# A mixture-of-experts layer on one core: the second pair's shared down product in seven half-products, one fetch of the expert lists, and a reordered start and routing

## The chip, the cores and the metric

The kernel runs on one core of one Trainium2 chip. The metric is the time of one execution on the device in microseconds, smaller is better. Before the change the median of nine runs is 1002.9 us (1000.19 to 1004.2).

The core has five engines with queues of their own: PE (matrix products into PSUM, the accumulator memory of eight banks), DVE (vector arithmetic), ACT (scalar functions, copies and casts), POOL (constants, indirect transfers) and SP (here only issues transfers). Each works through its queue in order and waits on semaphores for the others. Transfers run on 16 DMA engines beside them.

## What is computed

Inputs: `x` (8 batches of 256 rows of 1024, so T = 2048 tokens), one adapter number for each batch, eight adapter matrices of 1024 x 1024, and the weights of a mixture of 16 experts with a shared expert. Cut to what matters:

```python
w = weight[adapter_ids]
y = jnp.einsum('bsi,boi->bso', x, w)              # cond: one adapter matrix per batch

gu_s = y @ shared_w_gate_up.T                     # 1024 -> 2 * 1024
g_s, u_s = jnp.split(gu_s, 2, axis=-1)
shared_out = silu(g_s) * u_s @ shared_w_down.T    # 1024 -> 1024

probs = softmax(y @ gate_w.T)                     # 16 experts
topk_vals, topk_idx = top_k(probs, 2)             # two experts per token, weights normalised
...                                               # each expert: 1024 -> 2*256, silu(g)*u, 256 -> 1024
out = x + moe_out + shared_out
```

Only the two chosen experts of each token are computed, with fixed capacities for each expert in order of load (`CAPS`, 256 to 304 rows); what overflows goes through a conditional tail that is not entered here.

## The kernel before

**Precision.** Every product is in float32 quality: a float32 matrix is split into a high part and a low part in PE's reduced float32 type (`split`, lines 79 to 81: ACT casts the high part, DVE subtracts to get the low one), and a product is three matmuls, high x high, high x low, low x high (`mm3`, lines 103 to 106; the same three in `product`, line 425). So each weight tile that is loaded (`load_w`, line 89: a 512 KB load on SP into one of four staging tiles `st`, then `split` into one of five tiles `hl`) costs one cast on ACT and one subtraction on DVE.

**Work that is tucked between loads.** `between` is a list; each call of `load_w` takes its first entry and queues that work behind the subtraction of this load on its engine (lines 97 to 100, `issue_after`). The program is otherwise traced in order and a scheduler sets the order of each engine's queue by a simulated timeline, so the trace's order can differ from that of the lines where dependences allow it.

**Stages, in order of time.**

- `cond(b)` (line 209), eight times: y = x_b times its adapter matrix; two loads of x and eight of the matrix, 96 matmuls of 128 x 512. Results leave to DRAM (`y_d`) on ACT's queue.
- The shared gate/up product for a pair of token groups (four groups of 512 tokens: groups 0 and 1 are the first pair, 2 and 3 the second) is class `Up` (line 374): Strassen's scheme over the pair in stages `stage_a` to `stage_d`, with sums of the inputs in `sums` and of the weights in `sums_b` and `sums_d`. The first pair's sums of weights are stored in DRAM (`ss_d`) for the second. The first pair's stages alternate with `cond(3)` to `cond(7)`. y is read back (`y_block`, line 344, on POOL's queue) and transposed on DVE (line 178). `ring` holds four tiles of split operands. PSUM banks are taken in turn from seven (`bank`, line 75); the eighth bank is `psm`, for small things.
- `route(g, parts)` (line 236) for each group: 16 matmuls for each column part against the gate weights into `lp`, softmax, the two best experts, ranks, and eight indirect stores on POOL (line 333) that put token numbers and weights into a table `tab_d` in DRAM. For groups 1 to 3 the operands are split into `rb` tiles from the pool of `hl` (`parts_of`, line 363); for groups 2 and 3 the rows are transposed into the two halves of one tile `tt` first (`pair_work`, `transposed_pair`).
- After the last route: the order of the experts by load (lines 782 to 793), then `entries` (line 660): for each expert one small load of its token numbers (`tb`, line 670) and one of its weights (`cr`, line 671) on SP, first for the two first experts, later for the other 14. `places` makes gather indices of `tb` with a DVE transposition and four POOL additions (line 656); `weights` transposes `cr` on PE (line 683) into `ct`.
- `shared_down(g, h, ring, acc, dst)` (line 533): down product of one group: two halves of the output columns, four loads of `sd` each, 96 matmuls a half over four banks, then an addition into `acc` (line 554) and a store on SP (line 555). It runs for groups 0 and 1 here, while POOL gathers the rows of the first experts (line 579).
- Experts (lines 839 to 857): gathered rows, transposed, up product, down product.
- The second pair's `Up`, which reads the stored sums of weights, while `combine` (line 558) gathers and adds the expert rows for each group into `ca` tiles on POOL; then `shared_down(2, ...)` and `shared_down(3, ...)`, lines 894 and 895, and the kernel ends with the last four stores.

```python
    combine_kept(range(NB, 2 * NB))
    ...
    acc = combine(pc[1], range(2 * NB, 3 * NB), x)
    for u in range(4):
        up.stage_d(u)
    close(px)
    pd = pool("pd", 4)
    acc3 = combine(pd[1], range(3 * NB, 4 * NB), x)
    shared_down(2, G, ring, acc, out)
    shared_down(3, S_, ring, acc3, out)
```

Of the kernel before, what the change touches and what calls it, by code (L numbers as in the profile page):

```python
# [17 lines left out]
P = 128  # L18
B, S, H = 8, 256, 1024
T = B * S  # L20
# [3 lines left out]
G = 4  # L24
GT = T // G
# [5 lines left out]
SLOTS = T + CAP  # L31
# [6 lines left out]
def adapter_moe_kernel(ctx: ExitStack, tc: tile.TileContext, xT, x, itok, wc, gate, wgu, wd, sgu, sd, out):  # L38
# [45 lines left out]

    homes, loads, last_gather, marks = [whl], [0], [None], []
# [3 lines left out]
    def load_w(src, parts=1):  # L89
# [3 lines left out]
        for i in range(parts):  # L93
            cs = slice(i * 1024 // parts, (i + 1) * 1024 // parts)
            last_load[0] = nc.sync.dma_start(st[:, cs], src[:, cs])
            end = split(hl[:, 0, cs], hl[:, 1, cs], st[:, cs])
# [5 lines left out]

    def mm3(ps, lhs, rhs, first, last):
        nc.tensor.matmul(ps, lhs[0], rhs[0], start=first, stop=False)  # L104
        nc.tensor.matmul(ps, lhs[0], rhs[1], start=False, stop=False)  # L105
        nc.tensor.matmul(ps, lhs[1], rhs[0], start=False, stop=last)  # L106
# [4 lines left out]
    gpk = cpool.tile([P, NC * 2 * E + P], FR, tag="gpk", name="gpk")  # L111
# [3 lines left out]
    nc.sync.dma_start(it_sb, itok)  # L115

    ident = cpool.tile([2 * E, 2 * E], F32, tag="ident", name="ident")
# [9 lines left out]
    c1, c2 = (t[:, :, 1:2].bitcast(F32).rearrange("p a o -> p (a o)") for t in tid)  # L127
    msum = cpool.tile([P, E], BF, tag="msum", name="msum")
# [3 lines left out]
    def constants(ring):  # L132
        make_identity(nc, ident)
# [3 lines left out]
        nc.gpsimd.memset(ones, 1.0)  # L137
# [30 lines left out]
    def zeros(ys):  # L168
        zr = ys.tile([P, 1024], F32, tag="yr", name="zr")
        nc.gpsimd.memset(zr, 0.0)  # L170
        nc.sync.dma_start(y_d[T // P].rearrange("a p f -> p a f"), zr[:, :].rearrange("p (a f) -> p a f", a=4))
        nc.sync.dma_start(comb_d[T : T + P, :], zr[:, :E])
        nc.sync.dma_start(os_d[ZROW : ZROW + 16, :], zr[:16, :])
# [19 lines left out]
    def pair_work(tb, ys):  # L193
        tv = tt.rearrange("p k (b n) -> p (k b) n", b=4)
        r = [y_block(tb + k, ys) for k in range(2)]
        return tv, [lambda k=k: transpose_to(tv[:, :, k * P : (k + 1) * P], r[k], 4) for k in range(2)]

    def transposed_pair(tb, ys):
        tv, works = pair_work(tb, ys)
        for work in works:  # L200
            work()
        return tv


# [4 lines left out]
    def cond(b, rows):  # L209
        xt = [load_w(xT[b, :, 0, :], 2 if b == 0 else 1)]  # L210
        aid = nc.values_load(it_sb[0:1, b : b + 1], engines=(mybir.EngineType.SP,), min_val=0, max_val=NA - 1)
        yrow = [rows.tile([P, 1024], F32, tag="yrow", name=f"yrow{k}") for k in range(2)]
        for h in range(2):
            ps = [bank() for k in range(2)]
            for q in range(4):
                if h == 0 and q == 1:
                    xt.append(load_w(xT[b, :, 1, :]))
                w = load_w(wc[ds(aid, 1), h * 4 + q].rearrange("a p f -> p (a f)"), 2 if b == 0 and h == 0 and q == 0 else 1)
# [17 lines left out]
    def route(g, parts):  # L236
        lp = psm.tile([P, GT], F32, tag="sm", name="lp")
        n0 = 0
        for get, n in parts:
            for c in range(NC):  # L240
                for l in range(2):
                    nc.tensor.matmul(  # L242
                        lp[:, n0 : n0 + n],
                        gpk[:, c * 2 * E : c * 2 * E + P],
                        get(c)[l],
                        start=(c == 0 and l == 0),
                        stop=(c == NC - 1 and l == 1),
                    )
            n0 += n
# [3 lines left out]
        for k in range(NB):  # L253
            nc.tensor.transpose(lt[:, k, :], ls[: 2 * E, k * P : (k + 1) * P], ident)
# [108 lines left out]
    def parts_of(srcs):  # L363
        for src in srcs:
            t = []
            for k in range(2):
# [618 lines left out]
```

## Time and profile before

| what | value |
|---|---|
| median of nine runs | 1002.9 us |
| the profiled execution | 1004.28 us, its span from first to last instruction 1002.4 us |
| mean granted clock of PE | 0.997 |
| busy: PE, DVE, ACT, POOL | 980.0, 661.3, 532.0, 304.8 us |
| DMA | 252.45 MB, 252 GB/s over the span |
| matmuls 128 x 512: from one start to the next | 0.227 us at full pace |
| DVE subtraction, 128 x 1024 | 1.22 us |
| ACT cast, 128 x 1024 | 1.05 us |
| DVE addition of a bank, 128 x 512 | 0.69 us |
| ACT copy of a bank, 128 x 512 | 0.59 us |

How to read the profile's lines. A timeline line gives start, duration, engine, line, operation, written tile and read tiles, shapes, how many are merged, and in brackets the idle time of the engine before it and what ended it. Matmuls are pipelined, so the duration of one (0.39 us) is longer than its distance to the next. A line of waits gives who waited for whom, the total, how often and the longest. A line of a stretch gives its bounds and length, then for PE, PEld (weight load), DVE, ACT and POOL the busy time with the number of instructions, then PE's granted clock, the share of the DMA engines and GB/s. A group line gives busy time, mean ns of one, and the idle time of the engine before them.

### The profile page before, as it was taken

To read this page: it belongs to the slowest core of one execution; us is meant where nothing else is said; L and a number is where in the kernel's file an instruction comes from. 1 tells how busy PE (TensorE), PEld (TensorE's weight loads), DVE (VectorE), ACT (ScalarE), POOL (GpSimd) and SP (SyncE) were. 2 spreads that over 40 slices of the span, in tenths; PEclk is the share of its full clock that TensorE was granted. 3 is DMA by queue.
4 is the path that set the end of the run, shared out by engine and by line. 5 is a ranking of instruction groups with operands and counts; after the bars stand their busy time and mean duration, and the time that the engine had idled before them with its cause. 6 is when DMAs were issued, how large, how long until landed. Compare 5 with 4: busy or idle time off the path is not lost.

```text
span 1002.4 us, 14185 instructions
## 1 busy us (share of the span) xinstructions
PE 980.0 (98%) x5043; PEld 839.5 (84%) x5043; DVE 661.3 (66%) x886; ACT 532.0 (53%) x709; POOL 304.8 (30%) x312
## 2 busy tenths in 40 slices
PE   6989999999999999989999999999999999999997
PEld 4878878888888888879999999999998888888886
DVE  5567588565876786848878778878875324565531
ACT  4546466556553451416777767767665556233220
POOL 1000303000003003847885664650003352603200
PEclk9999999999999999999999999999999999999999
DMA  8988647979878134749988888888878999946931
GB/s 286 332 292 301 211 148 219 393 268 319 273 216 291 62 126 118 252 150 367 332 301 299 259 296 293 275 283 305 298 245 300 262 331 323 273 139 200 265 124 44
DMA packets 83783, 252.45 MB, mean 252 GB/s; under 512 B 13367, under 2 KB 22199, under 8 KB 83703
## 3 DMA queue, kind: packets, MB, share of 16 engines
q1 hardware_dynamic: 51526, 174.07, 50.9%
q0 software_dynamic: 19312, 60.47, 20.8%
q10 hardware_dynamic: 12864, 16.91, 4.6%
q8 instruction: 41, 0.67, 0.3%
q14 instruction: 40, 0.32, 0.1%
HBM read 203.17 MB, written 48.25 MB: 251 GB/s over the span
## 4 chain that ended last, share of the span: by engine, by line
PE 85%; DMA 4%; POOL 3%; issue 3%; DVE 2%; SPq 1%; ACT 1%; ACTq 0%; POOLq 0%; DVEq 0%
PE acc L425 28%; PE acc L105 18%; PE acc L106 18%; PE acc L104 18%; PE acc L647 2%; POOL yg L579 2%; DMA st<-wc 1%; DVE hl L81 1%; PE lp L242 1%; POOL tab_d L333 1%; DMA y_d<-yrow 1%; DMA raw<-sgu 1%; ACT hl L80 1%; DMA st<-xT 1%; SPq L670 0%
## 5 line engine op out<-in xcount | busy, mean ns | idle before, releaser
L81 DVE TENSOR_TENSOR hl<-st,hl 128x1024 fp32r<-128x1024 f32 (+1 forms) x254 | 304.9, 1208 | 177.5 <-ACT hl L80 176.6
L80 ACT CAST hl<-st 128x1024 fp32r<-128x1024 f32 (+1 forms) x254 | 263.0, 1042 | 200.3 <-PE acc L106 79.7
L425 PE MATMUL acc<-op,hl 128*128 128x512 f32 x1056 | 242.6, 390 | 0.7 <-DVE hl L81 0.7
L425 PEld LDWEIGHTS acc<-op,hl 128*128 128x128 f32 x1056 | 197.5, 188 | 41.9 <-DVE hl L81 1.1
L579 POOL DMA_INDIRECT yg<-y_d,ix x128 | 160.3, 1252 | 57.9 <-issue 33.2
L104 PE MATMUL acc<-yte,hl 128*128 128x256 f32 (+6 forms) x512 | 147.4, 288 | 0.0
L106 PE MATMUL acc<-yte,hl 128*128 128x256 f32 (+6 forms) x512 | 147.3, 288 | 0.0
L105 PE MATMUL acc<-yte,hl 128*128 128x256 f32 (+6 forms) x512 | 146.9, 287 | 0.0
L105 PE MATMUL acc<-hl 128*128 128x512 f32 x256 | 100.9, 394 | 3.6 <-DVE hl L81 3.6
L105 PE MATMUL acc<-hl,ht 128*128 128x512 f32 x256 | 100.4, 392 | 0.0
L106 PE MATMUL acc<-hl,ht 128*128 128x512 f32 x256 | 100.2, 393 | 0.0
L106 PE MATMUL acc<-hl 128*128 128x512 f32 x256 | 100.1, 391 | 0.0
L104 PE MATMUL acc<-hl 128*128 128x512 f32 x256 | 91.9, 394 | 8.2 <-ACT hl L80 8.2
L104 PE MATMUL acc<-hl,ht 128*128 128x512 f32 x256 | 99.6, 392 | 0.0
L105 PEld LDWEIGHTS acc<-yte,hl 128*128 128x128 f32 x512 | 96.4, 188 | 0.6
L104 PEld LDWEIGHTS acc<-yte,hl 128*128 128x128 f32 x512 | 96.4, 188 | 0.6
L106 PEld LDWEIGHTS acc<-yte,hl 128*128 128x128 f32 x512 | 96.2, 188 | 0.0
L347 POOL DMA_DIRECT2D yr<-y_d x24 | 13.3, 554 | 249.6 <-DMA y_d<-yrow 139.4
L425 PE MATMUL acc<-op,shl 128*128 128x512 f32 x288 | 66.7, 389 | 0.0
L104 PEld LDWEIGHTS acc<-hl 128*128 128x128 f32 x256 | 48.3, 190 | 19.2 <-ACT hl L80 9.3
L425 PEld LDWEIGHTS acc<-op,shl 128*128 128x128 f32 x288 | 54.1, 188 | 11.2
L105 PEld LDWEIGHTS acc<-hl 128*128 128x128 f32 x256 | 48.3, 189 | 16.1 <-DVE hl L81 6.3
(191 smaller groups left out, 1321.0 us busy)
## 6 DMA issues: line engine op xcount, KB each, us to landing
st<-wgu SPq DMA_DIRECT2D x64, 512.0 KB
st<-wc SPq DMA_DIRECT2D x63, 512.0 KB
st<-sd SPq DMA_DIRECT2D x32, 512.0 KB
st<-wd SPq DMA_DIRECT2D x32, 512.0 KB
os_d<-o SPq DMA_DIRECT2D x32, 512.0 KB
yr<-y_d POOLq DMA_DIRECT2D x24, 512.0 KB, 5.3
st<-sgu SPq DMA_DIRECT2D x24, 512.0 KB
st<-ss_d SPq DMA_DIRECT2D x20, 512.0 KB
```

Of the source, the lines that this page charges most:

```text
L80: nc.scalar.copy(hi, src)
L81: return nc.vector.tensor_tensor(lo, src, hi.bitcast(F32), op=ALU.subtract).ins
L104: nc.tensor.matmul(ps, lhs[0], rhs[0], start=first, stop=False)
L105: nc.tensor.matmul(ps, lhs[0], rhs[1], start=False, stop=False)
L106: nc.tensor.matmul(ps, lhs[1], rhs[0], start=False, stop=last)
L242: nc.tensor.matmul(lp[:, n0 : n0 + n], gpk[:, c * 2 * E : c * 2 * E + P], get(c)[l], start=(c == 0 and l == 0), stop=(c == NC - 1 and l == 1),
L333: i = nc.gpsimd.indirect_dma_start(out=tab_d[:, :], out_offset=bass.IndirectOffsetOnAxis(ap=sli[:, k : k + 1], axis=0), in_=tid[r][:, tb, ...
L347: nc.gpsimd.dma_start(r, y_d[tb].rearrange("a (i t) f -> (a i) (t f)", t=4))
L425: nc.tensor.matmul(ps, lhs[x], rhs[y], start=(first and c == 0 and i == 0), stop=(c == 3 and i == 2), skip_group_check=True)
L579: last_gather[0] = nc.gpsimd.indirect_dma_start(out=r[:, t * 256 : (t + 1) * 256], out_offset=None, in_=y_d.rearrange("k a p f -> (k a p) f"),
L647: nc.tensor.matmul(ps, a3[:, fi, :], w[fi][:, l, hs], start=(fi == 0 and l == 0), stop=(fi == 1 and l == 1))
```

## The change

The diff does the following.

- **Second pair's down product** (new class `DownPair`). The two groups of tokens and the two halves of the output columns make a 2 x 2 block product, with the inner dimension halved as well; it is done by seven half-products of 48 matmuls (Strassen's scheme in Winograd's form, with 15 sums) in place of eight. Sums of weights and activations are made on DVE (`t1`, `t2`, `s3` between the loads of stage D; the others inside `run`), results that two blocks share are copied from PSUM by ACT (`copies`) and either copied back into fresh banks as a start value or added by DVE (`add`). The sums use the tiles `raw`, which are free by then. The last block's four stores go on ACT's queue.
- **One fetch of the expert lists.** `entries` is called once: one indirect load on POOL brings 320 entries for each expert into `cr`, repeated on all partitions, with row numbers `column` made on DVE (four small instructions); one DVE transposition and one DVE addition make all gather indices `ix`. The weights' transpositions on PE are three in place of six and are queued behind the newest matmul. `tab_d` is padded to a multiple of 320 slots an expert.
- **The start.** Twelve matmuls on constants (`warm`) come first. The first x tile and the first weight tile are loaded in halves in the order x, w, w, x (`load_first`), and the second half of x is loaded before the third weight tile of the batch and not before the second.
- **Later transpositions, routing in parts.** `route` is cut into `route_part` (16 matmuls for half of a group) and the rest. For groups 1 and 2 the halves and the rest become entries of `between`; for group 2 the rows' transpositions do, too. The three stores of zeros go to POOL's queue. The first pair of loads for `sums_b(0)`, the gate weights and the table's start values are queued behind the newest load.

```diff
+    def load_first(xsrc, wsrc):
...
+        for k, i in ((0, 0), (1, 0), (1, 1), (0, 1)):
+            src, st, hl = pieces[k]
+            cs = slice(i * 512, i * 512 + 512)
+            with tc.issue_after(last_load[0].ins):
+                last_load[0] = nc.sync.dma_start(st[:, cs], src()[:, cs])
+            split(hl[:, 0, cs], hl[:, 1, cs], st[:, cs])
...
+    nc.gpsimd.memset(ones, 1.0)
+    warm = psm.tile([P, 4, P], F32, tag="sm", name="warm")
+    for k in range(12):
+        nc.tensor.matmul(warm, ones, ones[:, :].rearrange("p (o n) -> p o n", o=1).to_broadcast([P, 4, P]), start=True, stop=True)
...
-                if h == 0 and q == 1:
+                if h == 0 and q == 2:
                     xt.append(load_w(xT[b, :, 1, :]))
...
+    class DownPair:
+        def __init__(self, h, raw):
+            self.h = [[h[n][:, 4 * k : 4 * k + 4, :] for k in range(2)] for n in range(2)]
+            self.r = [raw[n][:, 4 * k : 4 * k + 4, :] for n in range(2) for k in range(2)]
...
+        def works(self):
+            return [lambda f=f, t=t: f(t) for f in (self.t1, self.t2, self.s3) for t in range(2)]
...
+            ps = banks4()
+            self.product(ps, operand(ring, a11), self.weights(0, 0), True)
+            for t in range(2):
+                self.s12(t)
+            copies(a11, ps)
+            self.product(ps, operand(ring, a12), self.weights(1, 0), False)
+            s2 = operand(ring, r[1])
+            w = [made(self.flat(3, t)) for t in range(2)]
+            add(0, 0, ps)
+            store(0, 0, nc.sync)
+            ps = banks4()
+            for k in range(NB):
+                nc.scalar.copy(ps[k], a11[:, k, :])
+            self.product(ps, s2, w, False)
+
+            for t in range(2):
+                q = slice(2 * t, 2 * t + 2)
+                nc.vector.tensor_tensor(a12[:, q, :], a12[:, q, :], r[1][:, q, :], op=ALU.subtract)
+            copies(r[1], ps)
+            s3 = operand(ring, r[0])
+            w = []
+            for t in range(2):
+                x, y = self.loaded(1, 1, t), self.loaded(0, 1, t)
+                nc.vector.tensor_tensor(x, x, y, op=ALU.subtract)
+                w.append(made(x))
+            self.product(ps, s3, w, False)
+            copies(r[0], ps)
+            ops = operand(ring, a22)
...
+            self.product(ps, ops, w, False)
+            s1 = operand(ring, a21)
+            w = [made(self.flat(2, t)) for t in range(2)]
+            add(1, 1, [r[0][:, k, :] for k in range(NB)])
+            add(1, 0, ps)
+            store(1, 0, nc.sync)
+            ps = banks4()
+            self.product(ps, s1, w, True)
+            s4 = operand(ring, a12)
+            w = self.weights(1, 1)
+            add(0, 1, [r[1][:, k, :] for k in range(NB)])
+            add(1, 1, ps)
+            store(1, 1, nc.sync)
+            self.product(ps, s4, w, False)
+            add(0, 1, ps)
+            store(0, 1, nc.scalar)
...
+        nc.gpsimd.indirect_dma_start(
+            out=cr.rearrange("e s o -> e (s o)").bitcast(I32),
+            out_offset=None,
+            in_=tab_d.rearrange("(e s) o -> e (s o)", s=ENTRIES),
+            in_offset=bass.IndirectOffsetOnAxis(ap=column, axis=0),
+        )
+        nc.vector.transpose(ib, cr[:, :, 0].rearrange("p (t i) -> p t i", i=32))
+        nc.vector.tensor_scalar(ix, ib.rearrange("p t n -> p n t")[:, :E, :].bitcast(I32), seg[:, 0:1], None, op0=ALU.add)
...
-    places, weights = entries(pe[1], [0, 1])
-    places()
+    weights = entries(pe[1], column)
     e0 = expert_rows(pa[1], 0)
-    between[:] = [None] * 4 + [weights]
     shared_down(0, G, ring, down_rows(0, ys), xs_d)
     rs = expert_rows(pa[1], 1)
-    places, weights = entries(pe[1], range(2, E))
     yt, works = expert_yt_work(pa[1], e0)
-    between[:] = [works[0], None, works[1], places, works[2], None, weights]
+    between[:] = [None, weights, None, works[0], None, works[1], works[2]]
...
-    for u in range(4):
+    down = DownPair((G, S_), raw)
+    up.stage_d(0)
+    between[:] = down.works()
+    for u in range(1, 4):
         up.stage_d(u)
     close(px)
     pd = pool("pd", 4)
     acc3 = combine(pd[1], range(3 * NB, 4 * NB), x)
-    shared_down(2, G, ring, acc, out)
-    shared_down(3, S_, ring, acc3, out)
+    down.run(2, ring, (acc, acc3), out)
```

The routing's new order in the stream of loads:

```diff
+    between[:] = [w[0], w[1], w[2], both(w[3], part(0)), part(1), lambda: route(1, lp)]
     up.stage_a(0)
     up.stage_a(1)
-    route(1, parts_of([raw[1][:, :, k * 2 * P : (k + 1) * 2 * P] for k in range(2)]))
+    up.stage_a(2)
     zeros(ys)
-    up.stage_a(2)
+    after_loads(lambda: up.sums_loads(0))()
     up.stage_a(3)
...
-    tv, w = pair_work(2 * NB, ys)
-    between[:] = [None, None, None, w[0], None, None, w[1]]
+    lp2 = logits()
+    w = group_work(lp2, 2, ys)
+    between[:] = [None, None, None, w[0], None, None, w[1], None, None, w[2], both(*w[3:]), lambda: route(2, lp2)]
     cond(6, ys)
-    route(2, parts_of(tv if k == 0 else transposed_pair(2 * NB + k, ys) for k in (0, 2)))
```

## The prediction

> **What bounds the kernel now.** I read the page's busy shares first, then the list of waits for the matmul engine alone, then stretches of the timeline around each wait, and last the stretch that the change rewrites. The first line of the page says that PE is the path:
>
> ```profile
> PE 980.0 (98%) x5043; PEld 839.5 (84%) x5043; DVE 661.3 (66%) x886; ACT 532.0 (53%) x709; POOL 304.8 (30%) x312
> ```
>
> 98% says that a gain must come from fewer matmuls or from PE's few gaps. The waits of PE, all of them (engine, line, what it waited for: total us, times, longest):
>
> ```profile
> PE acc L104 <- ACT hl L80: 8.2, 2, 7.4
> PE acc L105 <- DVE hl L81: 3.6, 5, 1.8
> PE ct L683 <- DMA cr<-tab_d: 2.5, 1, 2.5
> PE lp L242 <- DVE rb L81: 0.9, 1, 0.9
> PE acc L425 <- DVE hl L81: 0.7, 1, 0.7
> PE lp L242 <- ACT rb L80: 0.3, 1, 0.3
> ```
>
> 16.2 us in all, of which 7.4 lie before the first matmul. One matmul's price is not the 390 ns of the groups (matmuls overlap) but the distance between two starts. The timeline of PE around the `ct` wait shows both that and what a wait does to the pace:
>
> ```profile
> 440.49 0.39 PE L106 MATMUL acc<-hl,ht 128*128 128x512 f32 x1
> 440.71 0.39 PE L104 MATMUL acc<-hl,ht 128*128 128x512 f32 x1
> 443.63 0.42 PE L683 MATMUL ct<-ident,cr 16*128 16x16 f32 x3 [2.53 <-DMA cr<-tab_d]
> ...
> 446.06 0.63 PE L104 MATMUL acc<-hl,ht 128*128 128x512 f32 x1
> 446.48 0.63 PE L105 MATMUL acc<-hl,ht 128*128 128x512 f32 x1
> 446.91 0.63 PE L106 MATMUL acc<-hl,ht 128*128 128x512 f32 x1
> ...
> 448.44 0.39 PE L105 MATMUL acc<-hl,ht 128*128 128x512 f32 x1
> 448.66 0.39 PE L106 MATMUL acc<-hl,ht 128*128 128x512 f32 x1
> ```
>
> Normal pace: 0.227 us. After 2.53 us of idleness eight matmuls start 0.427 us apart, so this wait costs 2.5 + 8 x 0.2 = 4.1 us. After the 1.84 us gap before 72.69 the pace is 0.23 at once: the half pace comes somewhere between 1.84 and 2.53 us.
>
> **The change, part by part.** Durations are from the profiled execution (1004.28 us, span 1002.4); its own time lies 1.4 above the median of 1002.9, so I sum there and take 1.4 off at the end.
>
> *Seven half-products.* The stretch from 909 to 996 is the second pair's down product:
>
> ```profile
> 909.00:996.00 87.00, 87.00 (x385) 71.88 (x383) 32.44 (x35) 17.93 (x18) 15.78 (x12) 1.00 0.56 165
> ```
>
> PE (first pair after the length) never idles, DVE is busy 32.4 of 87 us, ACT 17.9. Its groups (busy us, mean ns of one, idle before):
>
> ```profile
> L104 PE MATMUL acc<-hl,ht 128*128 128x512 f32 x128 | 49.8, 389 | 0.0
> L81 DVE TENSOR_TENSOR hl<-st,hl 128x1024 fp32r<-128x1024 f32 x12 | 14.7, 1222 | 22.3 <-ACT hl L80 22.3
> L554 DVE TENSOR_TENSOR ca<-acc,ca 128x512 f32<-128x512 f32 x15 | 10.1, 687 | 21.0 <-PE acc L106 21.0
> ```
>
> DVE's 22 and 21 us of idleness here are the room for the new sums. The loops give 384 matmuls; seven products of 48 are 336. The 48 that go are worth 48 x 0.2267 = 10.9 us. What comes beside them: DVE gets 14 operand splits, 14 weight splits and 10 half sums of 128x1024 at 1.22 (46.4) and 24 additions at 0.687 (16.5): 62.9 us in 76.2 of PE. ACT gets 28 casts at 1.05 and 16 copies at 0.59: 38.8. Three sums in halves (6 x 1.22 = 7.3 us of DVE) go to stage D, where from 850 to 910 DVE is busy 37.8 of 60. So on the average both fit; the question is the tightest product. S's last part ends at 913.86 now (L518 starts at 913.18); the four halves of `s12` (4.9) and one weight split (1.2) behind it end at 920.0, which is 909 + 10.9, where the first product ends. The second product writes the first bank then and the third bank 2.7 us later, and each needs a copy of 0.59 that in turn needs `s12`'s half: slack 2 us. Where a product goes on in the banks just copied, a bank is full 18 matmuls (4.1 us) before the product ends, and the copy or addition takes 0.6 to 0.7: covered, as long as ACT's or DVE's queue does not hold something late ahead of it. If that cover is gone in one product, it costs what DVE is over: the first window is the fullest, 12.5 us of work if nothing of it was done before, against 10.9. Bounds for new waits 0 (the stretch above, idle 0) to 7 x 1.6 = 11.2; I take 0.5, near the row with no wait, since DVE's queue keeps 13 us free. Loads are 12 of 512 KB plus six in stage D against 16: DMA share there is 0.56. The tail behind the last addition (996.20) has the same four additions and stores, on ACT's queue, which has nothing else left. **-10.9 + 0.5.**
>
> The Trainium skill (TensorE: Matmul & The Clock Gate, A second HAM failure mode: psum-queue depth-cycling) speaks against this part: cycling through PSUM banks can let PE idle briefly so often that its clock falls and rises again. The granted clock from 755 to 909, where copies and seeds alternate with products in the same way, is 1.00 and PE waits for nothing; were the rule to bite with eight slow matmuls in each product, the part would gain 1.6 x 7 = 11.2 less.
>
> *One fetch of entries.* 32 small DMAs on SP go (28 of them from 430.2 to 442.5, which held the `wgu` loads until 444.6), two memsets and eight small POOL instructions; the six transpositions become three, put behind the newest matmul. The wait for `cr` goes with its slow matmuls: **-4.1**. What comes: four small DVE instructions (0.17 to 0.42 each), one indirect DMA on POOL (L579: 1.25 us to issue, 5.6 to land for 128 KB; this is 320 KB, and other indirect rows take up to 13.5), one DVE transposition (0.44 for 256 elements, so about 0.55) and one DVE addition. Before, the scatter ended at 395.3 and the first gather began at 402.1; now 396.6 + 1.3 + 5.6 to 13.5 + 1 is 404 to 412, 2 to 10 later. The transpositions of the first expert sit three loads (16 us) later too, and its first matmul starts at 456.4: hidden, 0. Without that cover it costs the lateness itself, at most 10. POOL's later gathers queue behind the fetch but no longer wait until 446 for the second list: earlier. Below nothing I see only the 0.4 of three transpositions.
>
> The Trainium skill (TensorE: Matmul & The Clock Gate, Part 1) puts the fall of the clock after an idle window of about 3.4 us. Here 2.53 us were enough for eight matmuls at 0.427 us, and the measurement decides; by the rule alone the term would be 2.5.
>
> *The start.* Timeline of PE:
>
> ```profile
> 7.40 1.22 PE L104 MATMUL acc<-hl 128*128 128x512 f32 x2 [7.40 <-ACT hl L80]
> ...
> 12.96 0.73 PE L104 MATMUL acc<-hl 128*128 128x512 f32 x2 [0.79 <-ACT hl L80]
> 14.22 0.50 PE L105 MATMUL acc<-hl 128*128 128x512 f32 x1 [0.53 <-DVE hl L81]
> ```
>
> 14 matmuls take 6.82 us where 3.17 would do: 3.65 lost, by slow matmuls until 10.86, then by loads. Twelve matmuls on constants from about 1.2 us on, at 0.427, end near 6.3 and leave about one us of idleness: the pace should be full (were they as slow as one whole slow matmul, 0.63, they would end at 8.8 and cost 1.4). Order of the loads: the second half of the input (512 KB, cast at 10.62) goes behind the second weights (cast at 11.87), so these come about 1.3 us earlier, and 1 MB of `S<-sgu` (12.8, 13.8) and the writes that follow leave this stretch, where the DMA share is 0.86. Bounds 0 and -3.65; I take **-2.2**, since only the loads' part is sure to limit. The gap of 0.42 at 36.56 hangs, by the chain of waits, on a DVE sum of that early pair: **-0.4**. The gaps at 59.3 and 72.7 (0.9 and 2.0 with what follows) hang on DVE holding a transposition whose `yr` lands late; its place among the loads stays: 0, bounds -2.9 and +1. The pair's two loads now go behind stage A's weights, around 135, where the DMA share is 0.44; the sums that need them come after 175: 0 (if late, one `raw<-sgu` landing, 6.6). The three zero stores go from SP to POOL's queue (0.53 each), which is idle from 160 to 240 but for 8 us: 0. Gate and table loads move by some tens of us, ahead of the route that needs them at 78: 0.
>
> *Routing in parts.* Same matmuls, set between loads. The gaps are 0.43 + 1.14 at 268 and 269 (half two's transpositions start only after half one's splits) and 0.87 at 134. Bounds -2.4 and, if a part takes two of five `hl` buffers from the loads at a bad moment, +2 (as at 72.7). I take **-1.2**, half, as the second group's last transpositions are still one bundle.
>
> Sum: -10.9 + 0.5 - 4.1 - 2.2 - 0.4 - 1.2 = -18.3; 1004.3 - 18.3 = 986.0, against the median 984.6. **I predict 984.6.**
>
> **Rivals.** (a) *Loads bound the start and the parts trade waits*: start 0, routing 0, the 0.4 stays; -10.4 - 4.1 - 0.4 = -14.9, 988.0. For it: DMA share 0.86 to 0.90 until 75 us. Against it: over 1 MB leaves. (b) *DVE becomes the bound in the down product*: 11.2 of new waits rather than 0.5, 995.3; half of it 990. For it: 62.9 of 76 us and an in-order queue in which a sum waits for a load; against: it runs ahead. (c) *Slower*: at the product boundaries PE waits for ACT's copies (four casts behind a late sum, or 4 x 0.59 = 2.4 plus an addition of 0.69) and each wait passes the length at which PE falls to half pace. One costs 2.5 + 1.6 = 4.1 as at 443; the six boundaries 24.6, in place of the 0.5: 984.1 + 24.6 = about 1009. It decides from 18.3 / 6 = 3.1 us a boundary. Against: four banks fill 1.36 us apart, and from 755 to 909 no such wait. (d) *The parts do not do what they say*: the scheduler puts the route's matmuls together again; only the 1.2 goes: 986.
>
> **How the numbers follow.** Forecast with (d) 0.65, (a) 0.15, (b) 0.13, (c) 0.07. The lower end takes all bounds: 10.9 + 4.5 + 3.65 + 0.4 + 2.9 + 2.4 = 24.8, 978; the upper reaches to most of (b): 994. The measurement tells 0.2% (2 us) from no change. All but (c) lie below that; of their 0.93 I leave 0.03 to a mix that cancels: faster 0.90, same 0.03, slower 0.07.
>
> **What would show it.** Right: the seven products take about 76 us and PE's wait list has nothing from them; no wait at `ct` and no 0.427 pace near 443; first real matmul near 7.2 and full pace by 12; the lines at 268 without idle. Wrong: PE waits on DVE `shl` or ACT copies after stage D, PEclk below 1.00 there, or a POOL fetch that PE's first expert waits for.

## The result, and the profile after

The changed kernel takes 1010.1 us (median of 20 runs, 1004.7 to 1017.4) and the kernel before 1003.4 (62 runs, 1000.1 to 1007.3): a ratio of 1.0071, 95% interval 1.0057 to 1.0084. It is slower by 7 us, where 18 us of gain were forecast.

PE is still the path: busy 978.3 of a span of 1007.3 us, at a mean granted clock of 0.992. The change takes 48 matmuls away, and PE's list of waits shows where more than their worth went (the first four of its entries):

```profile
PE lp L269 <- ACT rb L82: 4.6, 1, 4.6
PE acc L486 <- DVE X L569: 3.8, 2, 2.2
PE acc L127 <- ACT hl L82: 3.0, 3, 1.7
PE acc L127 <- DVE acc L619: 2.9, 2, 2.6
```

In the list of before the longest wait behind the first matmul is the one at `ct`, 2.5 us, and that one is gone. In its place stand these: a part of the routing (line 269, `rb`), a bank in the stages C and D that DVE frees late (line 569), the start (line 127 for ACT's `hl`), and a bank that the shared addition frees late (line 619).

The part that the forecast worked out at most length behaves as forecast. The stretch of the new down product:

```profile
924.80:1001.00 76.20, 76.20 (x337) 62.76 (x335) 52.32 (x58) 30.39 (x39) 16.64 (x12) 1.00 0.57 158
```

PE is busy all of the 76.2 us at clock 1.00, DVE 52.3 of them and ACT 30.4. The forecast's 62.9 and 38.8 count the product's whole work; of its 38 sums and splits on DVE and its 28 casts on ACT, seven of each are done before the first matmul, and the last additions come behind the last one. From its first matmul to its last the product takes 76.2 us, against 86.8 before. But it begins at 924.8 us and not at 909.0. **The kernel had lost 15.8 us before its main part began.**

Where, by the ends of stages in three profiled executions (us; the second changed one is the run a0 below). An end is the start of the ACT or DVE instruction that takes the stage's last result; the last two rows are starts of matmuls:

| stage ends | before | changed | changed, a0 |
|---|---|---|---|
| `cond(0)`, its last copy | 33.7 | 31.8 | 33.6 |
| `cond(3)` | 106.8 | 105.1 | 109.0 |
| stage A, first pair | 159.3 | 164.0 | 167.7 |
| second step of stage B | 203.1 | 209.9 | 213.6 |
| stage D, first pair | 362.2 | 372.1 | 373.2 |
| shared down product, groups 0, 1 | 460.6 | 470.1 | 472.1 |
| first matmul of the last down product | 909.0 | 924.8 | 925.3 |
| last matmul | 995.8 | 1001.0 | 1001.2 |

So there are four places: from 106 to 159, from 159 to 372, around 447 (a loss that takes the old one's place), and stage D of the second pair. The first changed execution also lost 3.6 us at the end of the experts, which a0 did not; it is left out of what follows. How far one execution can be trusted: before, e1 and e7 below are the same kernel up to stage D of the second pair, and their profiles differ by up to 2.2 us at the ends ahead of it.

### The profile page after: what moved, and what is told of

Read it like the earlier page. It is cut to its first block, busy times and chain, and to the rows that moved or that the text cites. A ratio compares the mean times of both kernels' runs of the same rounds, so it can differ in the third digit from the quotient of the medians.

```text
span 1007.3 us, 13998 instructions
## 1 busy us (share of the span) xinstructions
PE 978.3 (97%) x5004; PEld 832.9 (83%) x5004; DVE 684.9 (68%) x915; ACT 542.7 (54%) x729; POOL 312.4 (31%) x314
## 5 line engine op out<-in xcount | busy, mean ns | idle before, releaser
L83 DVE TENSOR_TENSOR hl<-st,hl 128x1024 fp32r<-128x1024 f32 (+1 forms) x244 | 293.1, 1210 | 142.8 <-ACT hl L82 141.0
L82 ACT CAST hl<-st 128x1024 fp32r<-128x1024 f32 (+1 forms) x244 | 252.5, 1041 | 143.5 <-PE acc L129 59.1
L362 POOL DMA_INDIRECT tab_d<-tid,sli x32 | 40.0, 1249 | 143.6 <-DVE ranks L355 108.9
L486 PE MATMUL acc<-op,shl 128*128 128x512 f32 x288 | 68.8, 397 | 4.3 <-DVE X L569 2.2
L127 PEld LDWEIGHTS acc<-hl 128*128 128x128 f32 x256 | 47.7, 188 | 14.2 <-ACT hl L82 4.4
L128 PEld LDWEIGHTS acc<-hl 128*128 128x128 f32 x256 | 48.0, 188 | 13.5 <-DVE hl L83 3.6
L129 PEld LDWEIGHTS acc<-hl 128*128 128x128 f32 x256 | 48.1, 188 | 9.7
L82 ACT CAST yte<-tt 128x1024 fp32r<-128x1024 f32 (+6 forms) x43 | 35.8, 865 | 35.5 <-DVE tt L210 35.5
```

What stands on the lines that cost most here:

```text
L82: nc.scalar.copy(hi, src)
L83: return nc.vector.tensor_tensor(lo, src, hi.bitcast(F32), op=ALU.subtract).ins
L129: last_product[0] = nc.tensor.matmul(ps, lhs[1], rhs[0], start=False, stop=last).ins
L362: i = nc.gpsimd.indirect_dma_start(out=tab_d[:, :], out_offset=bass.IndirectOffsetOnAxis(ap=sli[:, k : k + 1], axis=0), in_=tid[r][:, tb, ...
L486: nc.tensor.matmul(ps, lhs[x], rhs[y], start=(first and c == 0 and i == 0), stop=(c == 3 and i == 2), skip_group_check=True)
```

## The experiments

Kernels that ran on the same chip share its runs of the kernel before. The chips differ: on two of the five here the kernel before takes 1003 to 1004 us, on three 1028 to 1032. On those three every profile has a stretch between 425 and 515 us in which PE stands idle between one matmul and the next, up to 2.9 us at a time, and waits for nothing that the profile shows. The stretch from 460 to 490 us of run e1 (columns as in the stretch above; before has 200 matmuls there, at clock 1.00) and one of run e9 show it:

```profile
460.00:490.00 30.00, 15.31 (x54) 11.97 (x55) 6.54 (x10) 3.49 (x7) 15.41 (x17) 0.60 0.58 189
```

```profile
476.00:494.00 18.00, 12.46 (x68) 9.56 (x67) 10.02 (x14) 8.04 (x14) 13.50 (x12) 1.00 0.69 219
```

The granted clock does not make the gaps: in e1 they begin at 460 and the clock falls at 465, in e9 it stays at 1.00. What makes them is open.

Ratios from those chips therefore have wide intervals, and there I go by the ends of stages ahead of that stretch, against run e1, which is the kernel before up to stage D of the second pair.

### First set: one part alone, or one part undone

**e1, the half-products alone**, in the kernel before:

```diff
+    down = DownPair((G, S_), raw)
+    up.stage_d(0)
+    between[:] = down.works()
+    for u in range(1, 4):
         up.stage_d(u)
...
+    down.run(2, ring, (acc, acc3), out)
```

> The kernel before with only the seven half-products (and their six pieces of work in stage D). Theory 1 (the half-products keep what was forecast, the loss lies in the other parts): 384 - 336 = 48 matmuls of 0.227 us less, 10.9, and one wait of some 1.8 us in stage D, as the trace of the change has it at 894.7, so about 1003.4 - 9.1 = 994.3, ratio 0.991. Theory 2 (the sums, their loads and their splits shift the queues and pay the saving back): 0.998 to 1.002.

Measured 0.9946 (0.9903 to 0.9989), between the two. The product takes 75.9 us, but in stage D PE waits 3.75 us at 913.6 and then runs 13 matmuls at half pace, 6.5 us in all. 10.9 - 6.5 = 4.4, and the ratio says 5.6.

**e3, the moved loads undone**, in the changed kernel:

```diff
-            if u:
-                self.sums_loads(u)
+            self.sums_loads(u)
...
-    after_loads(lambda: up.sums_loads(0))()
```

> The changed kernel with one thing undone: the first pair's two loads go back into sums_b. Theory 1a (these loads, issued at 104.5 beside the y round trip of the first pair and not at 135, make the stalls at 136 and, by the order of the later loads, at 194): the stalls of 7.3 and 2.2 us go, about 1010.1 - 6 to - 9 = 1001 to 1004, ratio to the kernel before 0.998 to 1.001. Theory 1b (the routing in parts makes them, since POOL's scatters now stand ahead of the last gathers of y): no change, 1009 to 1011, ratio 1.006 to 1.008.

Measured 0.9992 (0.9948 to 1.0037). The stall of the routing shrinks to 2.1 us and eight slow matmuls, 4.0 in all, where the next two runs on the same chip have 10 to 11.

**e4, the routing whole again**, in the changed kernel:

```diff
-    between[:] = [w[0], w[1], w[2], both(w[3], part(0)), part(1), lambda: route(1, lp)]
+    between[:] = up.rows_work(1)
     up.stage_a(0)
     up.stage_a(1)
+    route_whole(1, parts_of([raw[1][:, :, k * 2 * P : (k + 1) * 2 * P] for k in range(2)]))
```

(and likewise for groups 2 and 3).

> The changed kernel with the routing of groups 1, 2 and 3 whole again, in its old places. Theory 1b (routing in parts is the cause): the stall of 7.3 us at 136 goes and the old gap of 0.9 there and 1.6 at 268 come back: 1010.1 - 5 = about 1005, ratio 1.002. Theory 1a (the moved loads are the cause): within 1.5 us of the changed kernel, ratio 1.006 to 1.009.

Measured 1.0158 (1.0095 to 1.0221), and the stall is still there: 7.3 us at 137.8, 10.5 with what follows. So the routing does not make it. The ratio is above both theories.

**e5, the old fetches of entries**, in the changed kernel (the function itself as before, with its 32 small loads):

```diff
-    weights = entries(pe[1], column)
+    places, weights = entries(pe[1], [0, 1])
+    places()
...
-    between[:] = [None, weights, None, works[0], None, works[1], works[2]]
+    between[:] = [works[0], None, works[1], places, works[2], None, weights]
```

> The changed kernel with the two old fetches of entries (32 small transfers on SP, two lists) back. Theory 1c (the single fetch lands so late that the stall of 4.4 us at 447 only takes the place of the 4.1 at the old ct wait): within 1 us of the changed kernel, ratio 1.006 to 1.008. Rival (the late fetch also delays the experts' rows up to the end of the experts, where another 3.6 us were lost): 1010.1 - 4 = 1006, ratio 1.003.

Measured 1.0162 (1.0102 to 1.0223). Neither case gives this number; the wait at `ct` (2.0 us at 419) and the stalls at 140 (6.2) and 198 (1.4) are in its profile. That e4 and e5 stand above 1.007 is either the chip or the undone parts' worth, and the times alone do not say which.

### Second set

**a0, the changed kernel again.**

> The changed kernel itself, unaltered, beside the next three on one chip, since the chip of the first four experiments runs the kernel before at 1032 and not at 1003. If the runs with the routing back (1.016) and with the entries back (1.016) stand where they do because both still have the moved loads, this one is at 1.012 to 1.018 there; if undoing those two parts cost time by itself, it is at 1.006 to 1.008 as in the first comparison.

It came to a chip where before takes 1003.3, so it does not answer its question; it gives 1.0060 (1.0033 to 1.0087) and a second profile, which I use in the table above.

**e6, loads and routing both back** (e3 and e4 together).

> The changed kernel with both the two moved loads and the routing of groups 1 to 3 back. Theory 1 (the moved loads make most of the stall at 136, the routing in parts the 4 us that were left of it when the loads alone were back): that stall falls to some 1.3 us as in the kernel before, the gap of 1.6 at 268 comes back; 2 to 3 us below the run with the loads alone back, ratio 0.995 to 0.998. Rival (what is left there is the later start of the gathers of y, whatever the routing does): no gain, ratio 0.999 or more.

Measured 1.0036 (1.0012 to 1.0060): more than theory 1 said, on the rival's side. At 203 us it is 1.2 us behind before where a0 is 10.5, so the stretch from 106 to 203 is repaired. But 2 to 4 us go at 330, where no part that I had named is at work, and 6.3 in stage D of the second pair.

**e7, the half-products alone, t2's subtractions later than its loads** (the edit is shown against e1):

```diff
-            return [lambda f=f, t=t: f(t) for f in (self.t1, self.t2, self.s3) for t in range(2)]
+            return [lambda: self.t1(0), lambda: self.t1(1), self.t2_loads, None, lambda: later(0), lambda: later(1)]
```

(`t2_loads` holds the two loads, `later(t)` the subtraction of `t2` and `s3`.)

> The kernel before with only the seven half-products, and in stage D the two loads of the sum t2 one slot of the loop, the subtractions two or three slots later. Theory 1 (DVE stood 11.0 us behind that landing, PE 3.9 and 13 matmuls at half pace, 6.5 in all): the stall goes, 6 us below the half-products alone, ratio about 0.989. Rival (the half-products' sums and loads cost elsewhere): as before, 0.994 to 0.996.

Measured **0.9911 (0.9878 to 0.9944)**, 993.5 us: 9.9 less than before, on the faster kind of chip, and near theory 1. The stall was DVE standing, in order, before one landing. In the changed kernel and then in e7 (timeline, idle time and its cause in brackets):

```profile
892.81 1.22 DVE L648 TENSOR_TENSOR raw<-raw 128x1024 f32<-128x1024 f32 x1 [8.86 <-DMA raw<-sd]
893.96 0.68 DVE L569 TENSOR_TENSOR X<-acc,X 128x512 f32<-128x512 f32 x1
894.56 1.22 DVE L83 TENSOR_TENSOR hl<-st,hl 128x1024 fp32r<-128x1024 f32 x1
```

```profile
881.14 1.23 DVE L584 TENSOR_TENSOR raw<-raw 128x1024 f32<-128x1024 f32 x1 [2.23 <-DMA raw<-sd]
```

Behind the subtraction of `t2` stands the addition of line 569, which frees a bank that PE needs. The load may go out only when the old content of its tile has been split, so it cannot be early; its subtraction has to be late.

**e8, the start alone**, in the kernel before, with the change's `load_first`:

```diff
+    for k in range(12):
+        nc.tensor.matmul(warm, ones, ...)
...
+            x0, w0 = load_first(lambda: xT[b, :, 0, :], lambda: weights(0))
...
-                if h == 0 and q == 1:
+                if h == 0 and q == 2:
```

> The kernel before with only the new start: twelve matmuls on constants, the first loads in another order, the second half of the input a step later. Theory 1 (the forecast's term, and the -1.9 us seen at 33 us in the changed kernel): 2 us less, ratio 0.998. Rival (the loads bound the start, as the forecast's case (a) had it): no change, 0.9995 to 1.0005.

Measured 1.0027 (1.0004 to 1.0050), the rival's case or a little worse. PE starts early and then waits longer, in the changed kernel:

```profile
1.01 4.68 PE L143 MATMUL warm<-ones 128*128 128x512 bf16 x12 [1.01 <-POOL seg L166]
6.53 0.73 PE L127 MATMUL acc<-hl 128*128 128x512 f32 x2 [0.85 <-ACT hl L82]
...
11.58 0.73 PE L127 MATMUL acc<-hl 128*128 128x512 f32 x2 [1.74 <-ACT hl L82]
```

and in e8, where this wait of 2.31 us is followed by eight matmuls at half pace:

```profile
12.22 0.73 PE L116 MATMUL acc<-hl 128*128 128x512 f32 x2 [2.31 <-ACT hl L80]
```

At 33 us e8 is 0.3 behind before. All twenty profiles say the same: the last copy of `cond(0)` starts at 32.5 to 34.9 us (median 33.3) in the eleven with the old start and at 31.8 to 34.3 (median 33.8) in the nine with the new one. ACT's casts, for which PE waits here, wait for landings in before and in the changed kernel. The loads set the start, and the warm matmuls only move the wait.

### Third set: the table

The stall at 330 in e6 led to the table. The changed kernel's POOL stores (`tab_d<-tid,sli`) land later, and so does the store of y that runs beside them. SP's queue holds `acc<-x` until that store has freed its tile, and behind it stands `raw<-sgu`, for which DVE waits. In the diff one line of constants does this: `SLOTS`, the places for each expert, goes from 2352 to 2560 so that rows of 320 divide it.

**e9, 2560 places in the kernel before**, nothing else:

```diff
-SLOTS = T + CAP
+SLOTS = 2560
```

> The kernel before with one number changed: 2560 places for each expert in the table of entries and not 2352, as the one fetch of the changed kernel needs it. In the quiet stretch from 110 to 142 the scatters into the table take 3.1 to 3.5 us to land in three kernels with 2352 and 5.5 to 6.0 in three with 2560. Theory 3 (the wider spacing makes the scatters land later, and stores and loads of y beside them): scatters at 5.5 to 6 there, the store of y at 305 lands 5 us later, a stall of 2 to 4 us at 330 and some at 130: 1003.4 + 2 to + 5, ratio 1.002 to 1.005. Rival (the scatters land later because more transfers run beside them in the changed kernel): no change, 0.999 to 1.001.

Measured 1.0079 (1.0046 to 1.0111), more than theory 3 said, and the stall is there. DVE and PE in e9:

```profile
325.57 1.23 DVE L456 TENSOR_TENSOR raw<-raw 128x1024 f32<-128x1024 f32 x1 [9.20 <-DMA raw<-sgu]
331.55 5.72 PE L425 MATMUL acc<-op,shl 128*128 128x512 f32 x24 [2.31 <-DVE X L504]
```

and in before, where PE has no wait there:

```profile
318.79 1.23 DVE L456 TENSOR_TENSOR raw<-raw 128x1024 f32<-128x1024 f32 x1 [5.09 <-DMA raw<-sgu]
```

At 460 us e9 is 7.2 us behind e1.

**e10, 2352 places in the changed kernel** (7 x 336):

```diff
-ENTRIES = -(-CAP // 32) * 32
+ENTRIES = 336
...
-        nc.vector.transpose(ib, cr[:, :, 0].rearrange("p (t i) -> p t i", i=32))
+        nc.vector.transpose(ib, cr[:, :320, 0].rearrange("p (t i) -> p t i", i=32))
```

> The changed kernel with 2352 places again (the fetch takes rows of 336 entries, 2352 = 7 x 336). Theory 3: scatters land in 3 to 4 us, the stall of 2 to 4 at 335 goes and 1 to 3 of those at 137 and 197: 3 to 6 us less than the changed kernel, ratio 1.001 to 1.004. Rival: no change, 1.006 to 1.007.

Measured 0.9974 (0.9940 to 1.0008), better than theory 3 said. No stall at 197 or 335 is left; those of the moved loads (4.2 and 1.1 us near 136) and of t2 (5.7 with its slow matmuls) are.

**e11, three parts mended:** e10, e3 and e7's order of `t2` in one.

> The changed kernel with three things mended: the two loads back in sums_b, the loads of t2 a slot earlier than their subtraction, the table at 2352. Theory (these three make the loss, 7 to 9 and 5 to 6 and 2 to 5 us by the last profile of the changed kernel, and the half-products' 10.9 stay): 1009.4 - 14 to - 20 = 989 to 995, ratio 0.986 to 0.992. Rival (one stall takes another's place further on): above 0.995.

Measured **0.9882 (0.9834 to 0.9930)**. The lowest ratio of the study, 12 us below the kernel before.

**e12, the routing in parts alone**, in the kernel before, for groups 1 to 3 as in the change:

```diff
-    between[:] = up.rows_work(1)
+    between[:] = [w[0], w[1], w[2], both(w[3], part(0)), part(1), lambda: route(1, lp)]
...
-    route(1, parts_of([raw[1][:, :, k * 2 * P : (k + 1) * 2 * P] for k in range(2)]))
```

> The kernel before with only the routing of groups 1 to 3 in parts between the loads. Forecast's term: -1.2 (bounds -2.4 and +2), ratio 0.9988. Theory 2 (PE, in order, stands at a part of the routing for a late gather of y where it had stage A to do, about 2 us and eight matmuls at half pace at 128, less 1.2 at 268): +1 to +3, ratio 1.001 to 1.003.

Measured 0.9964 (0.9921 to 1.0008), on the forecast's side. The two gaps at 268 in before, which cost 1.6 us together, are gone: PE goes from the routing straight into the next stage.

```profile
262.42 2.07 PE L227 MATMUL lp<-rb,gpk 128*128 128x256 f32 x16
264.32 5.63 PE L436 MATMUL acc<-op,hl 128*128 128x512 f32 x24
```

### Fourth and fifth set

**f1, 2576 places in the kernel before** (`SLOTS = 2576`).

> The kernel before with 2576 places for each expert, 16 more than in the wide table: the spacing of two experts' lists is then 20,608 bytes, where 2560 makes 20,480, which is five times 4,096, and 2352 makes 18,816. Theory 3a (what hurts is a spacing that is a multiple of 4,096): as the kernel before, 0.998 to 1.002. Theory 3b (what hurts is the larger table): as the wide table, 1.005 to 1.011.

Measured 1.0083 (1.0022 to 1.0144), but the profile has no stall at 330, DVE waits as in before, and half-way through the shared down product (415 us) it is 2.1 us behind e1, where e9 is 6.8. Time and profile disagree: the time is on theory 3b's side. The chip is one of the three with the gaps (22.7 us of them in this profile), and the run stays unexplained; hence f5 and f6.

**f2, the moved loads alone**, in the kernel before:

```diff
     up.stage_a(2)
+    with tc.issue_after(last_load[0].ins):
+        up.sums_loads(0)
```

> The kernel before with only the first pair's two loads moved ahead, behind the third step of stage A. The forecast: 0. Theory 1a (they go out at 105 and stand beside the round trip of y through the memory, whose late landing holds DVE and then PE): 3 to 7 us more, ratio 1.003 to 1.007. Rival (they cost only together with the routing in parts, for which PE waits in order): 0.999 to 1.002.

The time, 1.0032 (0.9943 to 1.0121), decides nothing. The profile does: level with e1 at 105 us (0.7 ahead), 5.8 behind at 163, and the stall of the changed kernel stands in a kernel whose routing is whole. SP's loads, the two gathers of y on POOL (the second with all eight scatters of the routing between them), DVE and PE in f2:

```profile
104.12 0.92 SPq L437 DMA_DIRECT2D S<-sgu  x2
...
115.33 0.53 POOL L347 DMA_DIRECT2D yr<-y_d  x1 [24.19 <-DMA y_d<-yrow]
...
126.14 0.59 POOL L347 DMA_DIRECT2D yr<-y_d  x1
...
130.56 1.25 DVE L178 STREAM_TRANSPOSE raw<-yr 128x1024 f32<-128x1024 f32 x1 [8.54 <-DMA yr<-y_d]
...
132.94 0.58 PE L242 MATMUL lp<-rb,gpk 128*128 128x256 f32 x1 [4.33 <-ACT rb L80]
```

and in before:

```profile
103.71 6.49 SPq L95 DMA_DIRECT2D st<-sgu  x4
...
113.73 0.53 POOL L347 DMA_DIRECT2D yr<-y_d  x1 [20.11 <-DMA y_d<-yrow]
...
120.08 0.59 POOL L347 DMA_DIRECT2D yr<-y_d  x1
```

The loads go out at 104, and y's store of the same moment lands 4 us later. The second gather, which before stood between the scatters, stands behind them. From y's second store to the second gather it is 12.4 to 12.7 us in all fourteen profiles whose loads are in their old place, and 20.0 to 22.1 in the six that have them moved (the changed kernel, a0, e4, e5, e10, f2): none lies between. Two things are in that: y's store lands 4 us later, beside the loads, and four more scatters, one every 1.3 us, go ahead of the second gather, an order that is fixed when the kernel is built. Both came with the move; no run takes them apart.

**f3, the one fetch of entries alone**, in the kernel before, with rows of 336 as in e10:

```diff
-    places, weights = entries(pe[1], [0, 1])
-    places()
+    weights = entries(pe[1], column)
...
-    between[:] = [works[0], None, works[1], places, works[2], None, weights]
+    between[:] = [None, weights, None, works[0], None, works[1], works[2]]
```

> The kernel before with only the one fetch of entries (rows of 336, so that the table stays at 2352 places) and what hangs on it. The forecast: -4.1, ratio 0.996. Theory 1c (a wait of the same length at the shared addition takes the place of that at ct, since the first expert's transpositions now bunch before it on DVE): 0, ratio 0.999 to 1.001.

Measured 0.9961 (0.9901 to 1.0021): undecided. The profile shows the wait at `ct` replaced by one at the shared addition, here first f3 and then the changed kernel:

```profile
434.40 0.79 PE L106 MATMUL acc<-hl,ht 128*128 128x512 f32 x1 [2.30 <-DVE acc L559]
```

```profile
447.17 0.50 PE L127 MATMUL acc<-hl,ht 128*128 128x512 f32 x1 [2.58 <-DVE acc L619]
```

Each is followed by seven to nine matmuls at half pace, as the one at `ct` was. But four profiles with the old fetches have a wait at the shared addition too, beside the one at `ct` (e1 2.1, e8 2.5, e9 2.3, f1 2.4 us), so it is not shown that the one fetch makes it.

**f4, half-products and routing in parts** (the edits of e7 and e12), in the kernel before.

> The kernel before with the half-products (t2's loads a slot early) and the routing in parts, and nothing else of the change. If the two add, -9.9 and -3.7: about 1003.4 - 13.6 = 990, ratio 0.9865, below the mended change (0.988). If the routing's gain was that of one chip only, 0.990 to 0.991.

Measured 0.9944 (0.9877 to 1.0010). The interval leaves out 0.9865, where the two gains would add, and holds 0.990 to 0.991. In the profile both parts keep what they had: product 76.0 us, no wait in stage D, no gap at 268.

**f5 and f6, tables of 3072 and of 2800 places**, in the kernel before (`SLOTS` alone, as in e9).

> The kernel before with 3072 places for each expert: a spacing of 24,576 bytes, six times 4,096. Theory 3a (a spacing that is a multiple of 4,096 makes the scatters and the stores of y beside them late): as with 2560, the store of y issued near 305 frees its buffer after 10 us or more and PE stalls near 330; ratio 1.003 to 1.010. Theory 3b (the larger table does it): more than with 2560, and more than the next one.

> The kernel before with 2800 places: a larger table than 2560, its spacing 22,400 bytes, no multiple of 4,096. Theory 3a: as the kernel before, the store of y in 7 to 9.5 us, no stall near 330, ratio 0.998 to 1.002. Theory 3b: at least what 2560 cost, 1.005 to 1.011.

Measured 1.0253 (1.0217 to 1.0289) and 0.9999 (0.9978 to 1.0020), side by side on a chip where before takes 1003.8. The larger table of f6 costs nothing, so it is the spacing and not the size. f5 costs more than theory 3a said: by PE's gaps 6.7 us from 126, 6.8 from 177, 8.0 from 337, 8.6 from 420 and 2.8 at 468. The median landing of the eight scatters between 110 and 142 us is 3.5 us in before (2352) and 5.5 in a0 (2560); in f5 and then in f6 it is the last number of

```profile
tab_d<-tid,sli POOLq DMA_INDIRECT x8, 7.4
```

```profile
tab_d<-tid,sli POOLq DMA_INDIRECT x8, 3.5
```

and in f5 PE stands at the place of e9's stall for

```profile
343.40 2.90 PE L425 MATMUL acc<-op,shl 128*128 128x512 f32 x6 [6.20 <-DVE X L504]
```

## Why the prediction was wrong

Term by term, in us; "by profile" is from the ends of stages or PE's gaps of single executions, "by time" from a ratio.

| step of the prediction | forecast | shown |
|---|---|---|
| seven half-products, 48 matmuls | -10.9 | -10.5 to -10.9 by profile in every kernel that has them; e7 -9.9 by time |
| new waits beside them | +0.5 | 0 inside the product (0.4 in e3); 1.9 (changed), 4.7 (a0), 6.5 (e1) in stage D by profile |
| wait at `ct` | -4.1 | about 0 by profile (f3, changed kernel); by time open |
| start | -2.2 | e8 +0.3 by profile at 33, +0.4 to +5 by time |
| gap near 36 us | -0.4 | gone in the six profiles with the loads moved, but also in ten of the fourteen without |
| routing in parts | -1.2 | e12 -1.8 by profile between 106 and 362 us; -3.7 by time, with no change inside the interval |
| two loads moved | 0 | f2 +6.5 by profile between 105 and 163 us |
| spacing of the table | not in the sum | e9 +7.2 by profile, +4.7 to +11 by time |

From a0: -10.9 + 4.7 + 0 + 0.3 - 1.8 + 6.5 + 7.2 = +6.0, and its last matmul starts 5.4 us later than that of before. The terms come from single runs of several chips and each may be off by some 2 us, so a sum that closes to half a us is partly chance; but the two largest losses are the two steps that had no price.

**The step that failed first** is "The pair's two loads now go behind stage A's weights, around 135, where the DMA share is 0.44 ... 0". They went out at 104.5 (108.3 in a0), beside the round trip of y through the memory, and this cost 6.5 us in f2, where nothing else is changed. "Behind the newest load" is a place in SP's queue, and SP works far ahead of PE: the line of before at 103.71 above has stage A's weights, which PE uses until 159, issued there. I had placed the loads by the time at which PE reaches those lines. The share of the DMA engines from 80 to 120 rose from 0.77 to 0.89 (0.91 in f2).

**The table's spacing** stood in the diff and in the description of the change ("padded to a multiple of 320 slots"), and the prediction priced the fetch and never the padding. No row of before could have given the price, but it deserved a bound. e9, e10, f5 and f6 show that it costs and that the size alone does not. That multiples of 4,096 bytes are the bad spacings rests on two of these against two others, and f1's time speaks against it.

**In stage D** I argued from a sum: DVE busy 37.8 of 60 us, so six more halves fit. They fit, but an instruction that waits for a load holds what stands behind it. The rule I had written for the product ("as long as ACT's or DVE's queue does not hold something late ahead of it") was not applied to the six pieces that I moved into stage D. e7 shows that their order alone is worth the loss.

**The wait at `ct`** went as said. I had seen that the first expert's transpositions come 16 us later, and called them hidden because PE's first use is at 456. What I left out is DVE's own queue: in f3 and in the changed kernel they stand before the shared addition, which frees the banks, and PE waits there instead. That the bunching makes this wait is argued, since e1, e8, e9 and f1 have the wait with the old fetches; f3's time leaves room for a gain of up to 10 us and for none.

**The start** ended as rival (a) had it: loads bound it.

**Right:** the count of DVE's and ACT's work for the product, no wait inside it (0.4 us in e3), no half pace between its banks, so the rule on PSUM cycling did not bite; the routing's direction. The slower rival (c) named a time near the one measured, but by waits at product boundaries, and there are none: that it is near is luck.

**Open:** f1's time; what makes PE's gaps on three chips; whether e11 or e7 is the fastest (their intervals overlap; both are below both kernels); what the zero stores on POOL's queue and the later gate loads cost, which no run tried alone; the loss of 3.6 us at the end of the experts in one profile of two.

## What to carry to other kernels

Price a moved transfer where its queue will issue it, and read that place from the queue's own timeline: here SP had issued by 110 us what PE used until 159. Where a sum or a copy goes into an engine with time to spare, ask what it waits for and what stands behind it, and put it a stage behind its load. A constant that changes a layout in memory is a part of the change like any other: give it a run of its own.

## What the runs showed of the hardware that was not expected

**Spacing of small scattered writes.** Eight-byte stores into sixteen lists land in 3.5 us when the lists lie 18,816 or 22,400 bytes apart, in 5.5 at 20,480 and in 7.4 at 24,576, and 512 KB stores beside them land later too: a store of y between 302 and 315 us frees its tile after 7.6 us in before, 10.4 in e9, 11.8 in f5, 7.3 in f6. The bad two are five and six times 4,096 bytes; 20,608 (f1) looks good by profile (its store takes 8.5 us) and not by time. The Trainium skill (DMA: Bandwidth & Descriptors, Latency and other measured facts) reports lost rate for dense copies whose rows lie megabytes apart and that padding the pitch by a few KiB restored it; it infers that memory channels coincide. Here the pitch is a hundred times smaller and the writes are scattered, so its case is not ours; no run here shows the mechanism.

**The half pace comes in steps of 3.41 us.** PE falls to 0.427 us a matmul after 2.31 and 2.58 us of waiting (e8 at 12, changed at 447), but not after 2.06 (changed at 194); in a0, two waits of 0.97 and 0.53 us near 92 are enough for eight slow ones. So the length of one wait does not decide, as the prediction's "between 1.84 and 2.53" has it. In the clock records of the twenty profiles there are 60 stretches at half clock, those at each kernel's start and end left out. Each lasts 3.41 us or a multiple of it, up to nine times, and ahead of 57 of them PE had been busy for less than half of the last 3.41 us. Of 5669 such steps behind which the clock stayed full, 10 were less than half busy. The step ahead of the fall in before, and the step at half clock:

```profile
440.88:444.29 3.41, 0.88 (x5) 0.65 (x5) 0.63 (x1) 0.00 (x0) 0.31 (x1) 1.00 0.16 25
444.29:447.70 3.41, 3.41 (x9) 2.65 (x8) 0.72 (x3) 0.00 (x0) 2.93 (x5) 0.50 0.89 288
```

The Trainium skill (TensorE: Matmul & The Clock Gate, Part 1) says that the activity window, of about 3.4 us, runs freely and is not tied to the kernel, which agrees with this; that the clock falls after an idle window does not quite, since here a window that was less than half busy is enough.

**Chips differ by 25 us, most of it in one stretch.** On three of five chips PE stands idle between matmuls for a while in or behind the shared down product, in every kernel, for nothing that the profile shows; by PE's gaps and the half pace that follows this costs 9 to 27 us. Comparisons there need the ends of stages ahead of it.
